# A two-layer graph network on one core: a written-out order of all operations is replaced by another

## The chip, the cores and the metric

The kernel runs on one core of a Trainium2 chip. The time is the device time of one execution in microseconds, the median of the runs shown. TensorE, VectorE, ScalarE, GpSimd and SyncE (DMA issues) each run their own instructions in the order in which the program gives them.

## The reference

The input x has 64 graphs of 256 nodes with 256 features, and adj an integer adjacency matrix of 256 x 256 for each graph. Two layers follow each other, and no graph meets another.

```
# layer 0: attention with relations
q, k = x@Wq + bq, x@Wk + bk                      # 8 heads of 32
attn = softmax(q @ k^T / sqrt(32))
out  = sum over r in 0..3 of (attn * (adj == r)) @ (x@Wv[r] + bv[r])
x = layernorm(x + out@Wo + bo)
x = layernorm(x + gelu(x@W1 + b1)@W2 + b2)       # 256 -> 1024 -> 256
# layer 1: two graph attentions, then feed-forward
for W, a in (W1', a1), (W2', a2):
    Wh = h@W;  e = leaky_relu(Wh@a[:256] + (Wh@a[256:])^T, 0.2)
    h = softmax(where(adj > 0, e, -9e15), axis=1) @ Wh
h = layernorm(x + h)
out = layernorm(h + relu(h@w_ff1 + b_ff1)@w_ff2 + b_ff2)
```

All arithmetic is float32.

## The kernel before, in words

One graph is one pass through 215 named operations, each a few instructions on one engine. A dictionary PLACES gives every operation of graph 0 a place, a number on an imaginary axis of microseconds; graph g has the same operations at PERIOD = 60 further on for each graph. All operations of all 64 graphs are sorted by place and written in that order (lines 738 to 743, under tc.manual_schedule()). So PLACES is nothing but an order: each engine executes its share of the sorted list one after the other, and the framework adds the waits that the data and the buffers need. A graph's places reach over several periods, so about seven graphs are in work at once: while one is read in, others are in attention, in the first feed-forward, in graph attention and in the second feed-forward.

The operations, by the letters that the text uses. A digit pair is group of four heads (m) and head (h) or chunk.

- load, cast, jT, mask0 to mask4, xT: x and adj are read by SyncE (five transfers), adj is cast on GpSimd, transposed by DMA, and compared with 0 to 3 (mask0 to mask3) and 0 (mask4) on GpSimd; x is transposed on VectorE.
- qk, v, s (TensorE) with qkc (ScalarE) and vc (VectorE): queries, keys and values, and scores, four heads at a time.
- max, rec (VectorE), exp, nrm (ScalarE): softmax of one head. eT (VectorE) transposes its 32 x 32 squares; eW writes them to DRAM and eR reads them back transposed, both issued by SyncE. ec (ScalarE) copies them to a PSUM bank (pe), pm (VectorE, 128 x 1536) and pl (GpSimd) multiply them by the masks. po (TensorE) is the product with the values, oT its copy; wo the output product, ya its sum with the residual, y and yb the residual's read and bias.
- st (VectorE), rt and nb (GpSimd), ln (ScalarE), and for norms 2 and 4 also lg, lb (GpSimd): layer norms 1 to 4.
- a.. and b.. are the two feed-forwards, called ffa and ffb: T, W, R transpose their input as eT, eW, eR do; u0 to u3 are the up products, x0 to x3 their activation on ScalarE, S1 to S4 differences of blocks on GpSimd, d1 to d7 the seven block products of the down matrix, e1, e5, e6, e7 and e their sums into the residual on VectorE, g and r the residual itself.
- hT, hW, hR (VectorE, SyncE, SyncE) transpose the first layer's result; ga0, ga1 (TensorE) are the first graph-attention product, gac0, gac1 their copies. ipA, zA, zmA, zxA, zeA, zdA are its scores, leaky rectifier, mask, maximum, exponential and division (zd is a reciprocal on VectorE and a scaling on ScalarE); h10, h11 the product, h1c its copies; ipB to zdB and h2, h2a the second attention.
- store writes the result.

Buffers are rings by tag. The products qk, v, po, wo, up, ga, ip, h1, h2 and d2 to d4 share two PSUM banks (tag mm, line 121), each free again when the operation that empties it is done. Four banks hold the scores, one pe, one the other four block products. The squares (tag sq) have three buffers, the transposed heads (eT) three.

Besides the graphs' operations three lists have places: the weights' reads on SyncE (LOAD_PLACE, one each LOAD_STEP), and the preparation of the weights of the first feed-forward, of the graph attention and of the second feed-forward (FFA_PLACE, GAT_PLACE, FFB_PLACE).

Of the kernel before, what the change touches and what calls it, by code (L numbers as in the profile page):

```python
# [25 lines left out]

PERIOD = 60.0
PLACES = {
    "load": 53.867, "cast": 97.493, "xT": 97.71, "qk0": 104.245, "qkc0": 106.9, "qk1": 119.672,
    "jT": 125.369, "qkc1": 125.559, "s0": 132.678, "max00": 140.518, "mask0": 141.136, "exp00": 142.758,  # L30
    "max01": 146.96, "max02": 148.02, "exp01": 150.777, "max03": 151.795, "exp02": 152.317,
    "rec00": 155.303, "exp03": 155.868, "v00": 155.904, "s1": 156.815, "rec01": 157.829, "rec02": 158.727,
    "nrm01": 159.842, "vc00": 160.216, "nrm02": 161.802, "max11": 161.859, "y": 164.73, "nrm00": 166.521,
    "eT01": 170.012, "max12": 170.188, "rec03": 171.372, "max13": 172.776, "nrm03": 173.676,
    "mask1": 174.748, "eT02": 174.962, "v01": 176.86, "eW01": 178.226, "mask2": 178.72, "exp11": 178.845,
    "exp13": 181.003, "vc01": 181.985, "eR01": 182.242, "eT03": 183.28, "eW02": 184.007, "max10": 184.378,
    "eR02": 184.784, "eT00": 185.682, "rec13": 186.046, "v10": 188.279, "exp12": 188.643, "rec11": 188.711,
    "exp10": 188.805, "mask3": 189.4, "rec12": 189.445, "nrm11": 189.698, "ec01": 190.244, "eW00": 190.751,
    "rec10": 192.438, "eT11": 193.076, "pm01": 193.141, "ec02": 193.235, "eR00": 193.339, "v11": 193.431,
    "vc10": 193.581, "vc11": 194.438, "pl02": 194.965, "nrm12": 198.135, "pm02": 198.356, "pl01": 198.886,  # L40
    "nrm10": 199.125, "eW03": 199.313, "ec00": 199.435, "pl00": 199.871, "eR03": 200.251, "eW11": 200.817,
    "nrm13": 201.713, "pm00": 203.767, "ec03": 203.968, "pm03": 204.13, "eT10": 204.663, "eR11": 205.899,
    "eT12": 206.287, "pl03": 206.79, "eW10": 209.302, "po0": 211.653, "eW12": 212.494, "eT13": 213.145,
    "mask4": 213.241, "oT0": 214.947, "eR10": 216.339, "pl11": 216.59, "ec11": 218.123, "pm11": 220.7,
    "eR12": 224.889, "yb": 226.434, "pl10": 228.258, "ec10": 228.372, "eW13": 229.644, "pm10": 230.476,
    "pl12": 232.012, "ec12": 232.733, "pm12": 233.972, "eR13": 234.313, "ec13": 237.646, "pm13": 243.245,
    "pl13": 244.342, "po1": 250.956, "oT1": 252.88, "wo": 255.663, "ya": 259.532, "st1": 263.955,
    "rt1": 267.947, "nb1": 268.416, "ln1": 268.951, "aT": 271.243, "ag": 274.747, "aW": 277.829,
    "aR": 278.673, "ar": 281.381, "au0": 286.043, "ax0": 287.596, "au1": 287.634, "ax1": 288.43,
    "au2": 290.21, "ax2": 291.522, "au3": 291.667, "aS1": 292.473, "ax3": 294.535, "ad1": 295.258,  # L50
    "aS2": 295.665, "aS4": 296.531, "ae1": 300.808, "aS3": 301.199, "ad5": 301.799, "ad2": 302.493,
    "ad3": 303.25, "ad6": 303.473, "ad4": 304.153, "ad7": 304.802, "ae6": 306.99, "ae": 307.007,
    "ae5": 310.654, "ae7": 310.829, "st2": 311.642, "rt2": 311.927, "nb2": 312.331, "ln2": 312.385,
    "lg2": 312.54, "lb2": 312.827, "hT": 316.295, "hW": 321.721, "hR": 322.436, "ga0": 324.446,
    "ga1": 327.351, "gac0": 327.988, "gac1": 328.62, "ipA": 328.64, "zA": 329.126, "zmA": 330.316,
    "zxA": 331.133, "zeA": 333.29, "zdA": 334.704, "h10": 336.089, "h1c0": 338.792, "h11": 340.441,
    "h1c1": 341.113, "ipB": 342.954, "zB": 344.83, "zmB": 345.246, "zxB": 345.394, "zeB": 347.408,
    "zdB": 348.854, "h2": 354.906, "h2a": 355.066, "st3": 359.521, "rt3": 359.942, "nb3": 360.337,
    "ln3": 361.345, "bT": 366.354, "bW": 370.407, "bR": 371.452, "bu0": 375.17, "bx0": 377.213,
    "bu1": 379.925, "bx1": 381.424, "bg": 381.467, "br": 381.616, "bu2": 381.993, "bu3": 382.236,  # L60
    "bS1": 382.83, "bx2": 383.199, "bd1": 383.914, "bx3": 385.532, "bd5": 387.758, "be1": 388.574,
    "bd2": 389.18, "bS2": 389.426, "bd3": 390.223, "bS4": 391.414, "bd4": 393.372, "be": 395.332,
    "bd6": 400.691, "bS3": 401.147, "be5": 401.254, "be6": 406.262, "bd7": 409.8, "be7": 410.516,
    "st4": 441.003, "rt4": 446.204, "nb4": 456.718, "ln4": 477.36, "lg4": 485.49, "lb4": 490.083,
    "store": 498.629,
}
LOAD_PLACE, LOAD_STEP = 122.0, 3.0
FFA_PLACE, GAT_PLACE, FFB_PLACE = 255.0, 262.0, 264.0

# [702 lines left out]
```

## Time and profile before

| | |
|---|---|
| median of 3 runs | 3732.0 us (3729.56 to 3735.53) |
| profiled execution | 3735.23 us, of which the span 3733.5 us |
| granted TensorE clock, mean | 0.982 |
| TensorE busy | 3527.7 us (94%) |
| GpSimd, VectorE, ScalarE busy | 2796.0, 2691.9, 2560.1 us |
| transfers | 457.94 MB, mean 123 GB/s |

The page of a profile counts the busy time of each engine over the whole span. Because the order is periodic, it is read best in one period of the middle: the timeline of each engine shows start, duration, the line of the kernel, the operation with its tiles, and in square brackets how long the engine stood idle before it and what ended that. The list of waits adds these up by pair: engine, line, what was waited for, total us, times, longest us. SPq is SyncE's queue of DMA issues; an L304 there is a write of squares (eW, aW, bW, hW), an L308 a read of them (eR, aR, bR), L320 is hR.

### The profile page before, as it was taken

Reading aid. Unit: us, or ns where it says so; the run is one execution under the profiler, and the core shown is the slowest. Engines: PE = TensorE matmul, PEld = TensorE weight load, DVE = VectorE, ACT = ScalarE, POOL = GpSimd, SP = SyncE. Lnnn points to the kernel's source line nnn. Section 1 sums busy time; section 2 is a strip of 40 time slices with the busy share of each in tenths; the row PEclk is TensorE's granted clock in tenths of the full one; section 3 lists DMA queues with packets and bytes.
Section 4 is the critical chain, followed back from the end, with each engine's and each line's share of the span. In section 5 each row is a group of like instructions: output and inputs, shape, how many; then the busy total and the mean of one; then the engine's idle time right before and its main releaser. Section 6 shows DMA issues by size and latency. Waiting matters only on the chain.

```text
span 3733.5 us, 72960 instructions
## 1 busy us (share of the span) xinstructions
PE 3527.7 (94%) x25944; PEld 2767.2 (74%) x25944; DVE 2691.9 (72%) x4756; ACT 2560.1 (69%) x6917; POOL 2796.0 (75%) x3014
## 2 busy tenths in 40 slices
PE   5799999999999999999999999999999999999985
PEld 3577777777777777777777777777777777777775
DVE  4677777777777777777777777777777777777752
ACT  4567677777667767767767767767777767767752
POOL 3477787787787787787787777777787787787774
PEclk8899999999999999999999999999999999999998
DMA  6434444444444444444444444444444444444320
GB/s 171 127 117 130 123 123 130 125 124 128 123 124 128 126 122 128 126 124 126 126 125 125 129 119 128 126 121 128 126 122 128 126 125 125 126 122 128 115 80 29
DMA packets 809885, 457.94 MB, mean 123 GB/s; under 512 B 334256, under 2 KB 718896, under 8 KB 809520
## 3 DMA queue, kind: packets, MB, share of 16 engines
q1 hardware_dynamic: 809520, 453.27, 41.1%
q8 instruction: 205, 3.36, 0.4%
q14 instruction: 160, 1.31, 0.1%
HBM read 243.42 MB, written 201.33 MB: 119 GB/s over the span
## 4 chain that ended last, share of the span: by engine, by line
PE 77%; DMA 10%; POOL 4%; DVE 3%; issue 2%; ACT 2%; SPq 2%; POOLq 0%; ACTq 0%; DVEq 0%
PE ffa_ps L380 11%; PE po L560 10%; PE v_ps L492 9%; DMA hT<-hT_d 7%; PE ffa_po L415 6%; PE qk_ps L473 6%; PE ffb_ps L380 5%; PE ffb_pq L415 5%; PE ffb_po L415 5%; PE ffa_pq L415 5%; PE ga_wps L590 4%; PE h_ps L635 3%; PE h_ps L649 3%; PE s L508 3%; DMA hT_d<-hT_sq 3%
## 5 line engine op out<-in xcount | busy, mean ns | idle before, releaser
L543 DVE TENSOR_TENSOR pm<-rel,pe 128x1536 f32<-128x1536 uint8 x512 | 892.4, 1743 | 212.2 <-ACT pe L539 162.5
L548 POOL TENSOR_TENSOR pl<-rell,eT 128x512 f32<-128x512 bf16 x512 | 589.3, 1167 | 164.2 <-PE po L560 112.0
L531 ACT ACTIVATE e<-e,rden 128x256 f32<-128x256 f32 x1024 | 455.6, 503 | 119.1 <-DVE rden L526 119.1
L492 PE MATMUL v_ps<-wv,xT 128*128 128x512 f32 x1024 | 490.9, 602 | 4.7 <-DVE v L499 3.4
L521 ACT ACTIVATE e<-s,nmax 128x256 f32<-128x256 f32 x1024 | 472.5, 477 | 22.9 <-DVE eT_sq L299 13.6
L380 PE MATMUL ffb_ps<-ffb_T,f 128*128 128x256 f32 x2048 | 465.8, 381 | 14.1 <-DMA ffb_T<-ffb_T_d 13.7
L380 PE MATMUL ffa_ps<-ffa_T,w 128*128 128x256 f32 x2048 | 463.7, 379 | 5.3 <-ACT ffa_h L388 5.3
L380 PEld LDWEIGHTS ffb_ps<-ffb_T,f 128*128 128x128 f32 x2048 | 390.4, 191 | 95.3 <-issue 43.8
L380 PEld LDWEIGHTS ffa_ps<-ffa_T,w 128*128 128x128 f32 x2048 | 383.7, 190 | 55.8 <-ACT ffa_h L388 6.3
L388 ACT ACTIVATE ffb_h<-ffb_ps,bf_c 128x256 f32<-128x256 f32 x512 | 217.1, 482 | 245.0 <-PE ffb_ps L380 244.9
L560 PE MATMUL po<-pm,v 128*32 128x256 f32 x6144 | 364.3, 385 | 18.5 <-DVE pm L543 17.9
L299 DVE STREAM_TRANSPOSE eT_sq<-e 128x512 f32<-128x512 f32 x512 | 350.3, 694 | 16.5 <-DMA eT_d<-eT_sq 14.4
L403 POOL TENSOR_TENSOR ffa_t<-ffa_h 128x512 f32<-128x512 f32 x64 | 81.8, 1278 | 371.6 <-ACT ffa_h L388 371.6
L513 DVE TENSOR_REDUCE nmax<-s 128x2 f32<-128x512 f32 x512 | 335.1, 664 | 6.0 <-PE s L508 6.0
L539 ACT COPY pe<-eT 128x512 f32<-128x512 f32 x512 | 304.8, 595 | 41.5 <-DVE pm L543 19.0
L560 PEld LDWEIGHTS po<-pm,v 128*32 128x32 f32 x6144 | 188.0, 111 | 190.3 <-issue 51.8
L357 ACT ACTIVATE ffa_res<-ffa_res,nb_x,rs_x 128x256 f32<-128x256 f32 x256 | 139.8, 593 | 238.7 <-POOL nb_x L352 238.7
L465 POOL TENSOR_SCALAR rel<-adT 128x512 uint8<-128x512 bf16 x192 | 289.0, 1506 | 12.0 <-DMA adT<-adb 12.0
L492 PEld LDWEIGHTS v_ps<-wv,xT 128*128 128x128 f32 x1024 | 175.4, 191 | 151.7 <-issue 124.6
L423 DVE TENSOR_TENSOR ffb_res<-ffb_po,ffb_res 128x256 f32<-128x256 f32 (+2 forms) x256 | 133.2, 521 | 207.6 <-PE ffb_po L415 140.1
L499 DVE TENSOR_TENSOR v<-v_ps,bv_r 128x512 f32<-128x512 f32 x256 | 176.5, 689 | 128.9 <-PE v_ps L492 122.9
L590 PE MATMUL ga_wps<-gext,hT 128*128 128x260 f32 x512 | 138.2, 416 | 110.0 <-DMA hT<-hT_d 110.0
(140 smaller groups left out, 7965.8 us busy)
## 6 DMA issues: line engine op xcount, KB each, us to landing
eT_d<-eT_sq SPq DMA_DIRECT2D x512, 256.0 KB, 2.3
eT<-eT_d SPq DMA_DIRECT2D x512, 256.0 KB, 3.1
xin<-in_x_dram SPq DMA_DIRECT2D x256, 64.0 KB, 3.6
adi<-in_adj_dram SPq DMA_DIRECT2D x64, 256.0 KB, 3.2
y<-in_x_dram SPq DMA_DIRECT2D x64, 256.0 KB, 3.2
ffa_T_d<-ffa_T_sq SPq DMA_DIRECT2D x64, 256.0 KB, 2.0
ffa_T<-ffa_T_d SPq DMA_DIRECT2D x64, 256.0 KB, 2.8
hT_d<-hT_sq SPq DMA_DIRECT2D x64, 256.0 KB, 3.2
```

The costliest lines, as they stand in the source:

```text
L299: nc.vector.transpose(self.sq.rearrange("p a c k y -> p (c k) a y"), src.rearrange("p c (k a x) -> p (c k) a x", k=KD, a=A))
L380: nc.tensor.matmul(p[:, f - f0, :], self.wa[:, k, f * P:(f + 1) * P], self.x.nodes(k), start=(k == 0), stop=(k == KD - 1))
L415: nc.tensor.matmul(self.p[bank][:, k], a[:, f], seven[self.name[:3]][i][:, f], start=(f == 0), stop=(f == KF // 2 - 1))
L465: nc.gpsimd.tensor_scalar(t.rearrange("p b c k y -> p (c k) b y"), self.adT.rearrange("p c k (b y) -> p (c k) b y", b=A), float(r), None, ...
L492: nc.tensor.matmul(p, self.xT[:, k, jc * P:(jc + 1) * P], wv[:, k, m].rearrange("p r n -> p (r n)"), start=(k == 0), stop=(k == KD - 1))
L513: nc.vector.tensor_reduce(self.nmax[m, h], self.s4[m][h].rearrange("p (c n) -> p c n", c=C), AX.X, ALU.max, negate=True)
L521: nc.scalar.activation(e[:, ic, :], self.s4[m][h][:, ic * N:(ic + 1) * N], AF.Exp, bias=self.nmax[m, h][:, ic:ic + 1], accum_out=self.den[ ...
L531: nc.scalar.activation(e[:, ic, :], e[:, ic, :], AF.Copy, scale=self.rden[m, h][:, ic:ic + 1])
L539: nc.scalar.copy(self.pe[m, h], self.et[m, h].t.rearrange("p b c k y -> p (b c k y)"))
L543: nc.vector.tensor_tensor(self.pm[m, h], self.rel.rearrange("p r b c k y -> p r (b c k y)"), bc(self.pe[m, h], [P, R - 1, C * N]), ALU.mult)
L548: nc.gpsimd.tensor_tensor(self.pm_l[m, h], self.rel_l.rearrange("p b c k y -> p (b c k y)"), self.et[m, h].t.rearrange("p b c k y -> p (b ...
L560: nc.tensor.matmul(po[hp, :], self.v[m][:, jc, r, hp], w, start=(r == 0 and jc == 0), stop=(r == R - 1 and jc == C - 1))
```

## The change

Only numbers change: the places of all operations, and those of the weights' reads and preparations. PERIOD stays at 60. The change is described as places found anew from a model in which transfers land in order and reads wait in SyncE's queue for their writes. The block products of the feed-forward (d1 to d7), which that description names too, are in both versions. From a graph's load to its store the places reach from 53.9 to 498.6 before and from 50.5 to 468.5 after. The core of the diff:

```diff
...
 PERIOD = 60.0
 PLACES = {
-    "load": 53.867, "cast": 97.493, "xT": 97.71, "qk0": 104.245, "qkc0": 106.9, "qk1": 119.672,
...
-    "nrm10": 199.125, "eW03": 199.313, "ec00": 199.435, "pl00": 199.871, "eR03": 200.251, "eW11": 200.817,
...
-    "eT12": 206.287, "pl03": 206.79, "eW10": 209.302, "po0": 211.653, "eW12": 212.494, "eT13": 213.145,
...
-    "aS2": 295.665, "aS4": 296.531, "ae1": 300.808, "aS3": 301.199, "ad5": 301.799, "ad2": 302.493,
...
-    "lg2": 312.54, "lb2": 312.827, "hT": 316.295, "hW": 321.721, "hR": 322.436, "ga0": 324.446,
-    "ga1": 327.351, "gac0": 327.988, "gac1": 328.62, "ipA": 328.64, "zA": 329.126, "zmA": 330.316,
-    "zxA": 331.133, "zeA": 333.29, "zdA": 334.704, "h10": 336.089, "h1c0": 338.792, "h11": 340.441,
-    "h1c1": 341.113, "ipB": 342.954, "zB": 344.83, "zmB": 345.246, "zxB": 345.394, "zeB": 347.408,
-    "zdB": 348.854, "h2": 354.906, "h2a": 355.066, "st3": 359.521, "rt3": 359.942, "nb3": 360.337,
-    "ln3": 361.345, "bT": 366.354, "bW": 370.407, "bR": 371.452, "bu0": 375.17, "bx0": 377.213,
...
-    "bS1": 382.83, "bx2": 383.199, "bd1": 383.914, "bx3": 385.532, "bd5": 387.758, "be1": 388.574,
...
+    "load": 50.469, "cast": 57.958, "jT": 95.84, "xT": 96.554, "mask0": 102.911, "mask1": 110.047,
...
+    "eR01": 157.633, "rec00": 157.8, "nrm00": 158.594, "eT00": 159.275, "nrm02": 159.922, "v01": 160.652,
...
+    "eW02": 170.328, "max10": 170.786, "nrm03": 171.325, "pl01": 171.348, "nrm11": 171.556, "eR00": 171.905,
+    "eT03": 172.223, "exp13": 172.85, "ec01": 172.891, "v10": 173.717, "vc10": 175.654, "rec12": 176.645,
+    "eT11": 177.037, "eW03": 177.436, "exp10": 178.092, "pm01": 178.674, "ec00": 179.248, "v11": 179.856,
+    "rec10": 180.535, "eR02": 180.538, "vc11": 180.966, "pl00": 182.451, "nrm10": 182.861, "pm00": 183.232,
+    "eT10": 184.014, "eR03": 184.212, "ec02": 186.356, "eW11": 186.418, "rec13": 187.778, "pm02": 188.384,
...
+    "eT12": 201.973, "mask4": 201.982, "oT0": 202.206, "pm11": 203.952, "eW13": 204.473, "eR10": 205.839,
...
+    "ln2": 296.499, "lg2": 298.191, "lb2": 298.532, "hT": 301.25, "hW": 306.094, "hR": 310.927,
+    "ga0": 312.907, "ga1": 313.044, "gac0": 313.944, "gac1": 314.043, "ipA": 315.499, "zA": 316.936,
+    "zmA": 319.507, "zxA": 320.243, "zeA": 321.567, "zdA": 321.6, "h10": 324.214, "h11": 324.414,
...
+    "zeB": 349.157, "zdB": 349.403, "h2": 349.965, "h2a": 351.453, "st3": 351.613, "rt3": 352.789,
+    "nb3": 353.038, "ln3": 354.94, "bT": 355.146, "bW": 357.939, "bR": 359.837, "bu0": 363.297,
...
+    "be": 384.147, "bS3": 385.351, "be1": 386.889, "bd6": 388.841, "bd7": 396.301, "be6": 396.573,
...
+    "lb4": 465.278, "store": 468.471,
...
-LOAD_PLACE, LOAD_STEP = 122.0, 3.0
-FFA_PLACE, GAT_PLACE, FFB_PLACE = 255.0, 262.0, 264.0
+LOAD_PLACE, LOAD_STEP = 97.0, 3.0
+FFA_PLACE, GAT_PLACE, FFB_PLACE = 253.0, 305.0, 308.0
```

What these numbers mean is seen when the places are taken modulo 60: the order that repeats in each period. In the lists below, worked out from the diff, the number after the point is the whole number of periods in the place: in period n the operation with .k is that of graph n - k. So two operations with different numbers belong to different graphs, and from the end of the list to its start the number of the same graph rises by one.

```
TensorE, before:
  ad5.5 ad2.5 ad3.5 ad6.5 ad4.5 ad7.5 v10.3 po1.4 s0.2 v11.3 bu0.6 wo.4 bu1.6 bu2.6 bu3.6 bd1.6
  ga0.5 ga1.5 bd5.6 ipA.5 bd2.6 bd3.6 po0.3 bd4.6 v00.2 h10.5 s1.2 h11.5 bd6.6 ipB.5 qk0.1 au0.4
  au1.4 bd7.6 au2.4 au3.4 h2.5 ad1.4 v01.2 qk1.1
TensorE, after:
  qk1.2 s0.2 bu0.6 bu1.6 bu2.6 bu3.6 bd1.6 ga0.5 ga1.5 bd5.6 ipA.5 po0.3 bd2.6 bd3.6 bd4.6 h10.5
  h11.5 v00.2 bd6.6 ipB.5 au0.4 au1.4 bd7.6 s1.2 au2.4 au3.4 v01.2 ad1.4 po1.3 ad5.4 ad6.4 h2.5
  ad2.4 ad3.4 ad4.4 ad7.4 v10.2 wo.3 qk0.1 v11.2
SyncE (DMA issues), before:
  eR01.3 eW02.3 eR02.3 jT.2 bW.6 eW00.3 bR.6 eR00.3 store.8 eW03.3 eR03.3 eW11.3 hW.5 hR.5 eR11.3 eW10.3
  eW12.3 eR10.3 aW.4 aR.4 y.2 eR12.3 eW13.3 load.0 eR13.3 eW01.2
SyncE (DMA issues), after:
  eR02.3 eR03.3 hW.5 eW11.3 hR.5 eR11.3 eW10.3 y.3 aW.4 eW13.3 eR10.3 aR.4 eW12.3 eR13.3 eR12.3 eW01.2
  jT.1 eR01.2 store.7 eW00.2 eW02.2 load.0 eR00.2 eW03.2 bW.5 bR.5
VectorE, after:
  st1.4 rec10.3 vc11.3 hT.5 pm00.3 eT10.3 rec13.3 pm02.3 aT.4 pm03.3 max01.2 eT13.3 max00.2 max02.2 zmA.5 zxA.5
  be5.6 zdA.5 eT12.3 rec01.2 max03.2 pm11.3 be.6 be1.6 vc00.2 pm10.3 zmB.5 eT01.2 rec02.2 pm13.3 zxB.5 xT.1
  be6.6 rec00.2 be7.6 pm12.3 eT00.2 eT02.2 max12.2 rec03.2 max11.2 st4.6 vc01.2 zdB.5 max13.2 rec11.2 ae1.4 max10.2
  ae6.4 h2a.5 st3.5 eT03.2 ae5.4 ae.4 ae7.4 st2.4 bT.5 vc10.2 rec12.2 eT11.2 ya.3 pm01.2
ScalarE, after:
  nrm10.3 qkc1.2 bx0.6 ec02.3 bx1.6 ln1.4 bx2.6 ec03.3 bx3.6 nrm13.3 gac0.5 gac1.5 ec11.3 zA.5 nrm12.3 exp01.2
  zeA.5 zdA.5 oT0.3 ln4.7 exp02.2 h1c0.5 nrm01.2 ec10.3 h1c1.5 exp00.2 zB.5 exp03.2 ec13.3 ax0.4 ax1.4 ec12.3
  ax2.4 nrm00.2 nrm02.2 ax3.4 exp12.2 zeB.5 exp11.2 zdB.5 oT1.3 nrm03.2 nrm11.2 exp13.2 ec01.2 ln3.5 ln2.4 exp10.2
  qkc0.1 ec00.2
GpSimd, after:
  pl00.3 rt1.4 bg.6 nb1.4 pl02.3 br.6 bS1.6 pl03.3 rt4.7 nb4.7 bS2.6 bS4.6 mask4.3 bS3.6 pl11.3 lg4.7
  ag.4 mask2.2 yb.3 pl10.3 mask3.2 pl13.3 pl12.3 mask0.1 aS1.4 aS2.4 ar.4 lb4.7 aS4.4 aS3.4 mask1.1 pl01.2
  rt3.5 nb3.5 rt2.4 nb2.4 cast.0 lg2.4 lb2.4
```

## The prediction

> **What bounds the kernel now.** I read the busy table first, then the waits of TensorE, then one period on each engine, then the ends of the span.
>
> ```profile
> PE 3527.7 (94%) x25944; PEld 2767.2 (74%) x25944; DVE 2691.9 (72%) x4756; ACT 2560.1 (69%) x6917; POOL 2796.0 (75%) x3014
> ...
> PE ga_wps L590 <- DMA hT<-hT_d: 110.0, 64, 9.0
> PE po L560 <- DVE pm L543: 17.9, 3, 9.2
> PE s L508 <- ACT e L521: 15.3, 4, 14.7
> ...
> 276.00:332.00 56.00, 54.34 (x405) 42.83 (x406) 42.20 (x76) 39.84 (x108) 43.95 (x48) 1.00 0.43 127
> ```
>
> TensorE is the bound: in a 56 us stretch of the middle it is busy 54.3, GpSimd 44, VectorE 42, ScalarE 40. It waits once per graph, always in the same place (64 times): the first product of the graph attention, ga0, waits for the transposed rows hT. All its other waits together are below that and lie at the two ends. Now one period, TensorE first, then the chain that makes hT, then SyncE's queue (SP):
>
> ```profile
> 1206.70 1.06 PE L415 MATMUL ffa_po<-w,ffa_h 128*128 128x128 f32 x8
> 1207.60 1.88 PE L492 MATMUL v_ps<-wv,xT 128*128 128x512 f32 x4
> ...
> 1226.80 1.99 PE L590 MATMUL ga_wps<-gext,hT 128*128 128x260 f32 x8 [1.22 <-DMA hT<-hT_d]
> ...
> 1209.90 0.75 DVE L340 BATCH_NORM_STATS2 st_x<-ffa_res 128x6 f32<-128x256 f32 x2
> ...
> 1212.63 1.09 ACT L357 ACTIVATE ffa_res<-ffa_res,nb_x,rs_x 128x256 f32<-128x256 f32 x2 [2.12 <-POOL nb_x L352]
> ...
> 1215.16 1.27 POOL L327 TENSOR_TENSOR ffa_res<-ffa_res,be_r 128x512 f32<-128x512 f32 x1
> ...
> 1216.70 0.70 DVE L299 STREAM_TRANSPOSE hT_sq<-ffa_res 128x512 f32<-128x512 f32 x1
> ...
> 1218.71 0.36 SPq L308 DMA_DIRECT2D eT<-eT_d  x1
> 1219.17 0.44 SPq L304 DMA_DIRECT2D eT_d<-eT_sq  x1
> 1219.66 0.43 SPq L304 DMA_DIRECT2D hT_d<-hT_sq  x1
> 1222.88 0.67 SPq L320 DMA_DIRECT2D hT<-hT_d  x1
> ```
>
> TensorE leaves ad7, the last block product of the first feed-forward, at 1207.6 (where the next matmul starts) and gets to ga0 18.0 us later. The chain ad7, st2, ln2, lb2, hT, hW, hR, ga0 takes 19.2. Its squares are ready at 1217.4, but hW goes out at 1219.66: SP stands behind an eR (1218.71) that waits for a buffer which GpSimd's pl frees, and an eW. Those 2.3 us are more than the whole wait. Undisturbed periods are 55.6 us; from ga0 at 220.65 to ga0 at 3520.59 are 59 periods, 55.93 on average, because in a few the wait reaches 2.6 us and the clock then drops.
>
> **What the Trainium skill says.** "DMA: Bandwidth & Descriptors", section "Two DMAs through the same engine are not ordered", says that the issuing engine must wait for the first transfer's semaphore before it issues one that reads what the first wrote. So a read blocks all of SP until its write has landed; here hW to hR is 3.2 us, and an unhurried pair (ffb_T, 1205.56 to 1207.97) 2.4. The same page, "Anatomy of one DMA", puts some 2.0 us fixed on a transfer; the trace has 2.0 to 3.9. "TensorE: Matmul & The Clock Gate", section "HAM oscillation", warns of idle gaps over about 3.4 us; here a gap of 2.61 us (ga0 at 1002.59) was already followed by a stretch at 0.83, so the measurement decides.
>
> **The change part by part.** No instruction is added or removed; all that changes is the order on each engine. I rank the places modulo 60, which gives each engine's order in one period, and walk it with start-to-start times from this trace. Let t be zero when TensorE leaves ad7. Pitches on TensorE: v 1.72, wo, qk, h2 and each up product 1.73, s 1.07, po 3.59, block product 0.89, ga0 with ga1 1.83, h10 or h11 0.97, ip 0.22. They sum to 53.6 per period; the trace without its wait has 55.57 - 1.42 = 54.15, so 0.5 are small gaps that I keep.
>
> *hT.* On TensorE the new order between ad7 and ga0 is v10, wo, qk0, v11, qk1, s0, four up products, bd1: 1.72+1.73+1.73+1.72+1.73+1.07+6.92+0.89 = 17.5 us, against 18.0 before, so the cover is no longer. The chain: ae7 ends 0.6, st2 1.6, root and offset (1.63) 3.3, ln2 4.4, lg2 and lb2 (1.24 each) 7.1. hT stands in VectorE's queue behind bT, vc10, eT11, ya, pm01 (1.67), st1 and vc11; vc11 waits for v11 (6.9 + 0.2) and ends 7.8, so hT ends at 8.4, sooner than before (9.8). The gain is in SP: before hW come bW (2.5), bR (4.9, after bW landed), eR02 and eR03 (5.3, 5.7), all gone by 6.1. hW goes at 8.5, behind nothing; hR 2.4 to 3.2 later, lands 3.9 on (this read's row): 14.8 to 15.6. ga0 is wanted at 17.5. **The wait goes, with 1.9 to 2.7 us to spare.**
>
> *bR, moved in front of hW.* bT needs ln3 (ends 1.1) and st2; bR lands 2.8 after 4.9, at 7.7; the first up product bu0 is wanted at 9.7 (before: much later). No wait, 2 us of slack.
>
> *The ring of two PSUM banks (tag mm).* Every product takes a bank that an evacuation two products earlier frees. Along the new order: qk0 (3.45) needs vc10, done 3.0; qk1 (6.9) needs qkc0, which stands behind ln2 and exp10, done 6.1; bu2 (13.2) needs bx0, 12.4; v01 (40.4) needs ax2, 39.6; h10 (26.7) needs zdA, 25.4; h2 (48.3) needs zdB, 46.7. One is late: **h11** (27.7) needs be, the add that empties the bank of bd2 to bd4. On VectorE be stands behind the reciprocal of zdA, eT12, rec01, max03 and pm11. ga0 ends 18.4; gac1 and ec11 by 20.3, zA 21.5, zmA and zxA 23.0, zeA (behind nrm12 and exp01) 24.2, reciprocal 24.4, eT12 25.0, max03 25.7, pm11 27.4, be 28.0. So TensorE waits about 0.35 us, and v00, bd6 and ipB behind it. Bounds: 0 if exp01 and nrm12 have run before zA, 1.0 if pm11 or zeA comes 0.7 later. I take 0.35. GpSimd's mask0 now waits for pm12 (40.0), which leaves pl01 at 51.7 and rt3 just on time (51.9): no cost, but no slack.
>
> So a period is 54.15 + 0.35 = 54.5: 59 x (55.93 - 54.5) = **84 us**. The low end without that wait is 59 x 1.78 = 105.
>
> *Fill.* The products ahead of the first ga0 are the same set before and after. In the chain of waits the preparation of the attention and second feed-forward weights stands alone from 97.8 to 117.7, 20 us (GAT_PLACE 262, FFB_PLACE 264). At 305 and 308 it falls between hT and ga0 of graph 0, where TensorE waited 9.0 us (165.39). I take that 9 as gain; bounds 17 (SP also comes to the first eW some 5 us sooner, as one group of loads less is ahead of it) and a loss of 5, if the new place holds up ga0. *Drain.* From the last hT on (3670.6 to 3733.5) one graph is alone and its chain is latency; two shorter slots before it may give 2. LOAD_PLACE: every weight is issued 25 places sooner, still ahead of its first use: nothing.
>
> Sum: 84 + 9 + 2 = 95 from the profiled execution's 3735.2 (span 3733.5 and 1.7 around it): 3640. The median of the three runs is 3.2 lower, 3732.0: so **3637**.
>
> **The rivals.**
> *Half given back.* Slacks of 0.45 (qk0 behind vc10), 0.75 (qk1 behind qkc0) and 0 (rt3) are as small as my latencies are rough; if 1.0 us more goes to such waits, the period is 55.5 and the time 3735 - 25 - 11 - 3 = 3696. For it: pm waits for pe 162.5 us in 192 places already. Against: in the walk VectorE idles 5 us between t = 10 and 24, which absorbs delays.
> *hT still late.* If SP is held at bR, eR02 or eR03 until hW goes at 12 (12 + 3.0 + 3.9 = 18.9 against 17.5), ga0 waits as before: 3732. Against: bT is ready by 2.3, and the buffers of both eR are free long before.
> *Slower: VectorE's queue takes the bound.* If zeA, and so everything through be, comes 2.5 us later than walked, h11 stops TensorE 2.85 us per period: 57.0, 59 x 1.07 = 63 lost, 11 gained at the ends, 3784. It decides from 1.8 us of stall at h11, where it equals what hT gives back. For it: ec02 is queued behind bx0, and pm02, pm03, max01 and zmA follow one another. Against: be would have to come 1.4 us later than the rows say.
>
> **How the numbers follow.** Forecast 0.62, half given back 0.15, hT still late 0.06, slower 0.17. A measurement of this kernel tells 0.2%, 7 us, from no change. Faster 0.77, same 0.06, slower 0.17. Range: the low end is 105 + 17 + 3 from 3732, 3607, and a little for clock drops that vanish: 3603; the high end takes in half given back and hT still late, 3736.
>
> **What would show it.** Right: ga0's wait for hT gone from TensorE's waits, periods of 54.2 to 54.9, hW's issue within 0.5 us of hT's end, a wait of some tenths at h11 (h_ps) on VectorE's ffb_res, first ga0 before 160. Wrong: 64 waits of over 1 us at any one TensorE line, above all h_ps, qk_ps or ffb_ps; periods over 55.9.

## The result and the profile after

The kernel after takes 3642.4 us (median of 4 runs, 3637.9 to 3643.7), the kernel before 3730.8 on the same chip (4 runs, 3728.2 to 3735.5): a ratio of 0.976, 95% interval 0.974 to 0.978, or 88 us. The profiled execution has 3637.9 us with a span of 3636.1; before these were 3735.2 and 3733.5.

The busy table of the kernel after, engine by engine:

```profile
PE 3537.1 (97%) x25944; PEld 2759.8 (76%) x25944; DVE 2685.0 (74%) x4756; ACT 2565.8 (71%) x6917; POOL 2795.3 (77%) x3014
```

The same instructions on every engine, in a span 97 us shorter. Now TensorE's waits of the kernel after (engine, line, what was waited for, total us, times, longest):

```profile
PE ffb_ps L380 <- DMA ffb_T<-ffb_T_d: 24.9, 4, 10.5
PE po L560 <- DVE pm L543: 15.5, 5, 5.4
PE qk_ps L473 <- DMA wq<-in_L_gnn_Wq_dram: 7.7, 1, 7.7
PE v_ps L492 <- DVE v L499: 7.5, 1, 7.5
PE s L508 <- ACT e L521: 5.7, 4, 2.8
```

ga0 no longer waits for hT; that row (110.0 us, 64 times) is gone from the list. What is left occurs one to five times, at the two ends. One period of the kernel after, from one ga0 to the next, in the table of stretches (TensorE, weight loads, VectorE, ScalarE, GpSimd):

```profile
1190.00:1244.68 54.68, 54.56 (x406) 42.75 (x405) 41.75 (x75) 39.94 (x109) 43.65 (x48) 1.00 0.43 129
```

TensorE is busy 54.56 of 54.68 us; the missing 0.12 is one gap, which is followed up below. The timeline of the same period shows the chain that used to be late, by engine:

```profile
1226.99 1.88 PE L492 MATMUL v_ps<-wv,xT 128*128 128x512 f32 x4
...
1244.68 1.92 PE L590 MATMUL ga_wps<-gext,hT 128*128 128x260 f32 x8
...
1234.69 0.70 DVE L299 STREAM_TRANSPOSE hT_sq<-ffa_res 128x512 f32<-128x512 f32 x1
...
1229.26 0.33 SPq L304 DMA_DIRECT2D ffb_T_d<-ffb_T_sq  x1
1231.32 0.37 SPq L308 DMA_DIRECT2D ffb_T<-ffb_T_d  x1
1231.78 1.01 SPq L308 DMA_DIRECT2D eT<-eT_d  x2
1235.42 0.33 SPq L304 DMA_DIRECT2D hT_d<-hT_sq  x1
...
1237.49 0.64 SPq L320 DMA_DIRECT2D hT<-hT_d  x1
```

TensorE leaves ad7 at 1226.99, the squares hT are ready at 1235.39, and hW goes out 0.03 us later. hR follows 2.07 us after hW and lands 4.1 us on, at 1241.6 (the median of this read is 3.8); ga0 takes it at 1244.68 with 3.0 us to spare, 3.3 in the median of 59 periods. Before, hW stood 2.3 us behind a read and a write.

The table compares all kernels of this study. The first two columns after the ratio are the starts of ga0 of graphs 0 and 1 in the trace, then the mean period over the next 59 graphs, then the time from ga0 of graph 60 to the end of the span. Each kernel is named by the experiment below.

| kernel | median us | ratio to before, 95% interval | ga0, graph 0 | graph 1 | period | rest |
|---|---|---|---|---|---|---|
| before | 3730.8 | | 165.4 | 220.7 | 55.93 | 212.9 |
| after | 3642.4 | 0.976 [0.974, 0.978] | 148.1 | 205.7 | 54.68 | 204.1 |
| e1_hw_early | 3658.0 | 0.981 [0.979, 0.982] | 162.0 | 215.5 | 54.71 | 207.4 |
| e9_zA_alone | 3731.2 | 1.001 [1.000, 1.001] | 163.3 | 218.6 | 55.94 | 209.8 |
| e7_hw_and_zA_early | 3611.4 | 0.968 [0.967, 0.969] | 161.2 | 215.0 | 53.98 | 209.7 |
| e10_hw_zA_weights | 3607.6 | 0.968 [0.967, 0.969] | 156.9 | 215.6 | 53.98 | 208.3 |
| e2_weights_late | 3724.8 | 0.999 [0.998, 1.000] | 156.4 | 216.6 | 55.85 | 209.3 |
| e3_both | 3655.7 | 0.980 [0.979, 0.982] | 156.1 | 214.6 | 54.74 | 210.7 |
| e5_weights_early | 3647.5 | 0.978 [0.976, 0.979] | 161.2 | 214.8 | 54.69 | 206.1 |
| e8_loads_late | 3637.6 | 0.975 [0.974, 0.976] | 147.8 | 205.9 | 54.68 | 206.1 |
| e6_hw_behind_eR11 | 3669.9 | 0.984 [0.982, 0.985] | 149.2 | 207.4 | 55.06 | 208.3 |
| e4_ae5_early | 3619.7 | 0.971 [0.970, 0.973] | 148.1 | 205.9 | 54.32 | 207.5 |
| e11_be_early | 3635.0 | 0.975 [0.974, 0.977] | 149.3 | 207.5 | 54.54 | 207.7 |
| e12_ae5_be_early | 3613.0 | 0.969 [0.968, 0.971] | 148.8 | 206.5 | 54.18 | 208.8 |

### The profile page after: what moved, and what is told of

Its sections match the earlier page's. It is cut to its first block, busy times and chain, and to the rows that moved or that the text cites. A ratio compares the mean times of both kernels' runs of the same rounds, so it can differ in the third digit from the quotient of the medians.

```text
span 3636.1 us, 73240 instructions
## 1 busy us (share of the span) xinstructions
PE 3537.1 (97%) x25944; PEld 2759.8 (76%) x25944; DVE 2685.0 (74%) x4756; ACT 2565.8 (71%) x6917; POOL 2795.3 (77%) x3014
## 4 chain that ended last, share of the span: by engine, by line
PE 95%; DMA 1%; DVE 1%; issue 1%; SPq 1%; ACT 1%; POOL 0%; POOLq 0%; ACTq 0%; DVEq 0%
PE ffb_ps L380 13%; PE po L560 12%; PE ffa_ps L380 12%; PE v_ps L492 12%; PE ffa_po L415 7%; PE ffb_po L415 6%; PE qk_ps L473 6%; PE ffb_pq L415 5%; PE ffa_pq L415 5%; PE s L508 4%; PE h_ps L635 3%; PE h_ps L649 3%; PE ga_wps L590 3%; PE wo_ps L580 3%; DMA eT<-eT_d 0%
## 5 line engine op out<-in xcount | busy, mean ns | idle before, releaser
L380 PEld LDWEIGHTS ffb_ps<-ffb_T,f 128*128 128x128 f32 x2048 | 388.2, 192 | 98.1 <-issue 43.9
L465 POOL TENSOR_SCALAR rel<-adT 128x512 uint8<-128x512 bf16 x192 | 287.3, 1497 | 215.9 <-DVE pm L543 183.7
L357 ACT ACTIVATE ffa_res<-ffa_res,nb_x,rs_x 128x256 f32<-128x256 f32 x256 | 139.7, 593 | 403.6 <-POOL nb_x L352 403.6
L388 ACT ACTIVATE ffb_h<-ffb_ps,bf_c 128x256 f32<-128x256 f32 x512 | 215.0, 471 | 210.5 <-PE ffb_ps L380 210.5
L492 PEld LDWEIGHTS v_ps<-wv,xT 128*128 128x128 f32 x1024 | 190.2, 191 | 144.5 <-issue 125.6
L388 ACT ACTIVATE ffa_h<-ffa_ps,b_c 128x256 f32<-128x256 f32 x512 | 207.3, 471 | 112.3 <-PE ffa_ps L380 111.6
L499 DVE TENSOR_TENSOR v<-v_ps,bv_r 128x512 f32<-128x512 f32 x256 | 172.4, 673 | 148.8 <-PE v_ps L492 148.7
L423 DVE TENSOR_TENSOR ffa_res<-ffa_po,ffa_res 128x256 f32<-128x256 f32 (+2 forms) x256 | 131.1, 512 | 190.6 <-PE ffa_po L415 183.7
L346 POOL TENSOR_SCALAR rs_x<-mv_x 128x2 f32<-128x2 f32 x256 | 56.9, 222 | 223.3 <-DVE mv_x L342 212.5
```

What stands on the lines that cost most here:

```text
L380: nc.tensor.matmul(p[:, f - f0, :], self.wa[:, k, f * P:(f + 1) * P], self.x.nodes(k), start=(k == 0), stop=(k == KD - 1))
L388: nc.scalar.activation(self.h[half][:, f1 + f, :], self.ps[f0][:, f, :], self.func, bias=self.ba[:, f0 + f:f0 + f + 1])
L492: nc.tensor.matmul(p, self.xT[:, k, jc * P:(jc + 1) * P], wv[:, k, m].rearrange("p r n -> p (r n)"), start=(k == 0), stop=(k == KD - 1))
```

## The experiments

The theory: ga0 waited because of SyncE's queue, not because of the work before it, and the 88 us are that wait less what the new order adds in smaller waits, and a shorter fill. The rivals: TensorE's order or the other queues made the gain; or the gain lies in the fill.

### hW alone in the old order

```diff
 before:
-"hT": 316.295, "hW": 321.721
+"hT": 316.295, "hW": 320.2
```

> The old order with one number changed: hW's place from 321.721 to 320.2, so SyncE issues the write of hT's squares ahead of the read eR03 (which waits for GpSimd's pl) and of the write eW11, not behind them. Theory (the wait at ga0 is made in SyncE's queue): hW goes out at once after hT, some 2 us sooner; hR then lands about 1 us before TensorE wants it; TensorE's wait for hT falls from 110 us to under 20, periods from 55.6 to 54.2, and the time from 3731 to between 3625 and 3655. Rival (the wait belongs to the chain of norm, GpSimd and VectorE, and only the whole new order mends it): ga0 still waits over 1 us per graph and the time stays within 10 us of 3731.

It took 3658.0 us: 71 of the change's 88 us from one number. The wait of ga0 for hT fell to 10.0 us in 3 graphs. The time is still a little above what was expected, and TensorE's waits name the reason:

```profile
PE po L560 <- ACT ga_z L609: 32.6, 59, 0.6
PE po L560 <- DVE pm L543: 17.4, 3, 8.4
```

po0 now waits in 59 graphs for the PSUM bank that zA empties. In the timeline of ScalarE and TensorE:

```profile
1258.10 1.09 ACT L357 ACTIVATE y<-y,nb_x,rs_x 128x256 f32<-128x256 f32 x2 [1.06 <-POOL nb_x L352]
1259.10 0.81 ACT L609 ACTIVATE ga_z<-ga_ips,ga_wh 128x256 f32<-128x256 f32 x2
...
1259.96 2.37 PE L560 MATMUL po<-pm,v 128*32 128x256 f32 x40 [0.44 <-ACT ga_z L609]
```

zA (L609) could start at 1257.7, when ipA ends, but stands in ScalarE's queue behind ln1 of another graph (L357), which itself waits 1.06 us for GpSimd. This is the wait that took the place of the one removed.

### zA alone, and with hW

```diff
 before:
-"ipA": 328.64, "zA": 329.126
+"ipA": 328.64, "zA": 328.7
```

> The kernel before with zA alone moved, from 329.126 to 328.7, so ahead of ln1 of the graph before on ScalarE; hW stays where it was. Theory: two limits lie one behind the other. While ga0 waits 1.4 us for hT in every graph, po0 has no wait that zA's place could take away, so nothing changes: 3722 to 3738, the wait of ga0 for hT stays at about 110 us. With hW moved as well the same edit was worth 46 us (3658 to 3611). Rival: ScalarE's order has a worth of its own, because everything behind zA comes 1 us sooner: 3690 to 3715.

Nothing changed: 3731.2 against 3728.9 for the kernel before on that chip. TensorE's waits have the old row:

```profile
PE ga_wps L590 <- DMA hT<-hT_d: 110.6, 64, 8.9
```

The same edit with hW's:

> The kernel before with two operations moved: hW from 321.721 to 320.2 (as in e1_hw_early, 3658) and zA from 329.126 to 328.7, ahead of ln1 of the graph before on ScalarE. In e1_hw_early po0 waited 0.55 us in 59 graphs for the PSUM bank that zA empties. Theory: ln1 in front of zA made that wait; with zA first it goes, 59 x 0.55 = 32 us: 3622 to 3632, period 54.1 to 54.3. ln1 then comes 0.5 us later, which nothing near needs. Rival: zA itself is late because ipA and the copies gac are, and po0 still waits 0.4 us or more, or the wait moves to the next product of the ring (bd2 for the bank of po0's other user): 3640 to 3660.

3611.4 us, 47 less than with hW alone and lower than the whole change by 31. The period is 53.98. The timeline shows why, zA now ahead of ln1:

```profile
1243.42 0.84 ACT L609 ACTIVATE ga_z<-ga_ips,ga_wh 128x256 f32<-128x256 f32 x2 [0.73 <-PE ga_ips L602]
1244.15 1.08 ACT L357 ACTIVATE y<-y,nb_x,rs_x 128x256 f32<-128x256 f32 x2
...
1245.10 2.80 PE L560 MATMUL po<-pm,v 128*32 128x256 f32 x48
```

and the table of stretches has no idle TensorE any more:

```profile
400.00:1000.00 600.00, 600.00 (x4476) 473.47 (x4475) 466.14 (x827) 444.53 (x1203) 484.73 (x522) 1.00 0.43 130
```

The size was underestimated: 59 x 0.55 = 32 us were expected, 59 x (54.71 - 53.98) = 43 came. po0's weight loads are late too, by up to 0.8 us (43.9 us in 59 graphs in the list of the kernel with hW alone), so the wait costs more than its 32.6 us. So two limits lay one behind the other, and the second was invisible until the first was gone: its edit is worth nothing alone and 47 us after the other.

### The weights' preparation and the weights' reads

```diff
 before:
-FFA_PLACE, GAT_PLACE, FFB_PLACE = 255.0, 262.0, 264.0
+FFA_PLACE, GAT_PLACE, FFB_PLACE = 255.0, 319.6, 319.7
```

> The old order with only the preparation of the graph attention's and the second feed-forward's weights moved: GAT_PLACE 262 to 319.6, FFB_PLACE 264 to 319.7, between hT and ga0 of graph 0. Theory (in the fill they stood alone on the chain for 20 us, and here fall into the 9 us wait for hT): the first ga0 comes 9 to 17 us sooner than 165.4, and the time falls by the same, to between 3712 and 3723; the steady periods stay at 55.6. Rival (the new place holds up ga0 by as much as the old one cost): the first ga0 between 160 and 170 and a time of 3726 to 3736.

The first ga0 came 9.0 us sooner, as forecast, the second only 4.0: about half is given back within one graph. In the time it is 4 us against the kernel before on that chip (3728.7), less than the theory expected and a little more than the rival did. The same edit with hW:

> The old order with both: hW at 320.2, GAT_PLACE 319.6, FFB_PLACE 319.7. Theory (the two parts act in different stretches and add up): the gain is the sum of those of the two single kernels within 5 us, 3610 to 3645, which would be as fast as the whole new order or faster. Rival (the weights' preparation now delays the sooner hT in the fill, so the second gain is lost): the time of the kernel with hW alone, within 4 us.

3655.7, only 2.3 below hW alone: the time is the rival's, the two don't add. The first ga0 is 5.8 us sooner than with hW alone, but the second only 1.0, so here too most is given back within one graph. And on top of hW and zA:

> The kernel before with hW at 320.2, zA at 328.7 and the preparation of the graph-attention and second feed-forward weights moved from 262 and 264 to 319.6 and 319.7, between hT and ga0 of graph 0. Theory: the first ga0 comes 5 us sooner (161 to 156), of which the next graph gives most back, as in e3_both, where it was worth 2.3 us: 3605 to 3611 against 3611 without it. Rival: with the steady part free of waits the whole 5 us stay: 3603 to 3606.

3607.6 (3605.1 to 3610.7) against 3611.4 (3609.9 to 3611.7): the second ga0 is no sooner (215.6 against 215.0), the ratios agree; the 4 us are not settled. It is the lowest median of this study. Then the reverse in the new order:

```diff
 after:
-FFA_PLACE, GAT_PLACE, FFB_PLACE = 253.0, 305.0, 308.0
+FFA_PLACE, GAT_PLACE, FFB_PLACE = 253.0, 258.0, 260.0
```

> The kernel after, with GAT_PLACE and FFB_PLACE back at 258 and 260, that is before the first feed-forward of graph 0 and not between its hT and ga0. If the new place of the weights' preparation is what brought the first ga0 from 165.4 to 148.1, the first ga0 comes 9 to 15 us later, 157 to 163, and the steady period stays at 54.7. Theory: about half of it is given back by the second ga0 (as 5 of 9 us were in the old order), so the total is 3645 to 3652, 0.1 to 0.25% above the kernel after (3642). Rival 1: all of it stays, 3651 to 3657. Rival 2: the place doesn't matter, because the earlier start of the whole pipeline gave the gain: first ga0 within 2 us of 148, total 3640 to 3645.

13.2 us later at the first ga0, 9.1 at the second: a part is given back within one graph, as the theory has it. At the ga0 of graph 60 it is still 9.5. The median is 5.2 us above the kernel after, which is inside the forecast, but the intervals of the two ratios overlap; between 5 and 10 us, what is left of it in the time is not settled. The reads alone:

```diff
 after:
-LOAD_PLACE, LOAD_STEP = 97.0, 3.0
+LOAD_PLACE, LOAD_STEP = 122.0, 3.0
```

> The kernel after with LOAD_PLACE back at 122, so that SyncE issues the weights' reads 25 places later; nothing else changes. In the old order the weights' preparation was worth 9 us at the first ga0, but the kernel after is 17.3 us sooner there; the other 8 are either the order of the operations or these reads. Theory (order): first ga0 at 147 to 150, total 3638 to 3646. Rival (reads): first ga0 5 to 9 us later, 153 to 157, total 3645 to 3652.

First ga0 at 147.8, time 3637.6: 4.8 below the kernel after, on another chip. The starts, the period and the rest differ by at most 2 us in the traces and the intervals of the ratios overlap, so no cost and no gain of the reads' place is shown.

### hW held in the new order

```diff
 after:
-"hT": 301.25, "hW": 306.094, "hR": 310.927
+"hT": 301.25, "hW": 312.2, "hR": 312.5
```

> The kernel after, with hW and hR put at 312.2 and 312.5: in SyncE's queue hW then stands behind eW11 and behind eR11, which can't be issued before eW11's squares have landed (2.1 to 3.2 us after eW11). Everything else keeps its order. Theory (the head of SyncE's queue decides when hT lands): hW 2.5 to 3.5 us later than hT's end, hR lands about that much later; of it 3.4 us of slack before ga0 are used up first, so ga0 waits 0 to 1 us per graph, and 59 periods give 0 to 60 us: 3640 to 3700, likeliest 3665, with a wait of TensorE's ga0 for hT in 20 to 64 graphs. Rival (hT has much more slack than 3.4 us, or SyncE's order isn't the cause): no waits for hT, 3638 to 3645.

3669.9, close to the likeliest 3665, with the wait back in 22 graphs:

```profile
PE ga_wps L590 <- DMA hT<-hT_d: 12.5, 22, 2.2
```

SyncE's queue in one period, where hT ended at 1241.78, and the ga0 that follows:

```profile
1239.27 0.45 SPq L304 DMA_DIRECT2D eT_d<-eT_sq  x1
1243.53 0.36 SPq L308 DMA_DIRECT2D eT<-eT_d  x1
1243.93 1.78 SPq L304 DMA_DIRECT2D hT_d<-hT_sq  x1
1247.80 0.64 SPq L320 DMA_DIRECT2D hT<-hT_d  x1
...
1251.59 1.99 PE L590 MATMUL ga_wps<-gext,hT 128*128 128x260 f32 x8 [0.35 <-DMA hT<-hT_d]
```

The read eR11 can't go before eW11 has landed (in the trace its wait ends with that, at 1243.40) and holds everything behind it for 3.8 us; hW goes 2.15 us after hT, and hR 3.87 after hW instead of 2.07. Landing 3.7 later, at 1251.5, it holds ga0 until 1251.59: the slack is used up. The period grows by 0.38, 22 us over 59. Only 12.5 are listed as this wait, but all of it lies at ga0: from the start of bd1 to that of ga0 59 periods take 71.7 us, against 52.6 in the kernel after, and ga0 with ga1 106.8 against 103.6. In 50 of the 59 ga0 starts within 0.3 us of hT's landing; in the kernel after it does so in none. The kernel keeps the new order otherwise, so it is the place in SyncE's queue that decides.

### The waits that the new order brings

The trace shows two places in each period at which TensorE starts late in the kernel after. The first is the last block product of the first feed-forward, ad7, in the timeline of TensorE, of its weight loads and of VectorE; the last line is ad4 of the kernel before, where ad7 follows at 1206.70:

```profile
1224.85 1.06 PE L415 MATMUL ffa_pq<-w,ffa_t 128*128 128x128 f32 x8
1226.03 1.13 PE L415 MATMUL ffa_po<-w,ffa_h 128*128 128x128 f32 x8
...
1226.00 0.97 PEld L415 LDWEIGHTS ffa_po<-w,ffa_h 128*128 128x128 f32 x8 [0.28 <-issue]
...
1225.50 0.38 DVE L423 TENSOR_TENSOR ffa_res<-ffa_po,ffa_res 128x256 f32<-128x256 f32 x1
...
1205.81 1.06 PE L415 MATMUL ffa_pq<-w,ffa_t 128*128 128x128 f32 x8
```

From ad4 to ad7 it is 1.18 us, where it was 0.89 before, the pitch of a block product. The add ae5 ends at 1225.88; ad7's loads start at 1226.00. ae5 reads another quarter of ad7's PSUM bank, and in the program ad7's first product carries a wait on VectorE. The trace calls the gap "issue" here, but in graph 0, here of the kernel with the weights early, it is long enough to be named (in the kernel after at 126.36, also 0.25 us):

```profile
145.77 1.13 PE L415 MATMUL ffa_po<-w,ffa_h 128*128 128x128 f32 x8 [0.25 <-DVE ffa_res L423]
```

The Trainium skill, "PSUM — Partial Sum Buffer", section "PSUM bank collisions raise a hardware error", gives a likely reason for such a wait: two engines must not access the same 32 partitions of one bank at once, even at different addresses, so a bank is guarded with its partitions and not by address. ad7 and ae5 both take all 128 partitions. No run here shows a collision; that the wait costs time, the next one does. ae5 needs ad5 only, which is long done; it stands behind h2a, st3 and eT03. So it was put ahead:

```diff
 after:
-"ae5": 292.42, "ad4": 292.531
+"ae5": 291.2, "ad4": 292.531
```

> The new order with one number changed: ae5's place from 292.42 to 291.2, so VectorE reads block product 5 out of the shared bank ahead of h2a and st3. Theory (in the new order d7 waits about 0.3 us per graph for ae5, since both use one PSUM bank): the start-to-start time from ad4 to ad7 falls from 1.18 to 0.9 us, periods from 54.68 to 54.4, the time by 15 to 18 us from 3642 to about 3625. Rival (d7 waits for the sum ae or the difference aS3, or h2a and its norm now come later by as much and qk0 waits instead): periods stay at 54.6 to 54.8 and the time within 5 us of 3642.

3619.7, 22.6 below the kernel after. The timeline of this kernel:

```profile
1218.54 1.06 PE L415 MATMUL ffa_pq<-w,ffa_t 128*128 128x128 f32 x8
1219.43 1.06 PE L415 MATMUL ffa_po<-w,ffa_h 128*128 128x128 f32 x8
```

0.89 again. 15 to 18 us were expected from the 0.29 alone; but ad7 itself also took 0.96 to the next product and now takes 0.89, so the wait was worth 0.36, the whole difference of the periods (54.68 to 54.32), 21 us. The longer product points to the weight loads: the first of ad7's eight matmuls takes 0.18 us to the next in the kernel after, each other one 0.11. The Trainium skill, "TensorE: Matmul & The Clock Gate", section "Step-by-step: what each phase is for", says that TensorE pulls a weight load ahead while the product before it still runs. A product that waits has lost that lead: ad7's loads start at 1226.00, 0.03 us ahead of it. That this is the reason was not tried apart from the wait.

The second place is h11, where the prediction put its wait. The list of waits of the weight loads has it:

```profile
PEld h_ps L635 <- DVE ffb_res L423: 19.6, 61, 0.3
```

and the timeline of TensorE has it at the first products of h10 and h11:

```profile
1199.33 0.38 PE L635 MATMUL h_ps<-ga_wh,ga_z 128*128 128x258 f32 x1
...
1200.29 0.48 PE L635 MATMUL h_ps<-ga_wh,ga_z 128*128 128x258 f32 x1
```

Four products of 0.22 would put h11 at 1200.21; it starts 0.08 later, and its first product takes 0.32 to the next (1200.61) instead of 0.22. h10 with h11 takes 1.93 us instead of 1.74. So be was moved ahead of pm11:

```diff
 after:
-"be": 384.147
+"be": 383.94
```

> The kernel after with the add be moved on VectorE from 384.147 to 383.94, that is ahead of pm11 and no longer behind it; nothing else moves. In the kernel after the weight loads of h11 wait 0.33 us for be in 61 graphs, and h11's four products start 0.09 us late and take 0.1 us longer: h10 with h11 takes 1.93 us instead of 1.74. Theory: that is the whole price of h11's wait; with be first it goes, 59 x 0.19 = 11 us: 3626 to 3636 against 3642, period 54.5. VectorE then stands 1.3 us before be for the last block product, and pm11 comes 1.8 us later, into a stretch where VectorE idles 2.2 us. Rival 1: the wait of the loads lies beside other work and costs nothing: 3638 to 3646. Rival 2: pm11's delay reaches the evacuation of v00 or the next heads and costs more than it gives: over 3646.

3635.0, 7.4 below the kernel after; the period falls by 0.14, h10 with h11 by the same (1.93 to 1.79). The loads still wait 0.2 us (11.2 us in 61 graphs). The wait is a cost, a little below the 11 us expected. Both edits:

> The kernel after with both edits: ae5 at 291.2 (as in e4_ae5_early, 3620) and be at 383.94 (as in e11_be_early). Theory: the two waits lie in different stretches of the period and add: 22 and 11 us below 3642, 3604 to 3612, period 54.1. Rival: with both gone another wait appears, as after hW's move, and only 22 to 26 us are left: 3616 to 3620.

3613.0: 29.4 below the kernel after, where the single edits gave 22.6 and 7.4. They add within the noise, as two waits in different stretches of the period should. The theory's sum (33) was 3 to 4 us too high because be gave less, so the time lies 1 us above its range; the rival's further wait did not appear. This version is as fast as the old order with hW and zA moved (3611.4), within 2 us; both beat the two kernels compared.

## Why the prediction was right, and where it was not

Forecast were 3637 us, measured are 3642.4. The sum was 84 + 9 + 2, for periods, fill and drain. The two profiled executions, which lie 97 us apart, give 74 + 15 + 9; the medians lie 88 apart, which leaves 14 for the two ends. So the mechanism was right, and that the total is only 5 us off is in part luck: the periods gave 10 us less than forecast, and the ends at least 3 more.

*hT and SyncE.* Right in mechanism and in nearly every time. Counted from the moment TensorE leaves ad7, hT ends at 8.4 (forecast 8.4), hW goes at 8.4 (8.5), hR at 10.5 (10.9 to 11.7), ga0 comes at 17.7 (17.5). The slack is 3.3 us against 1.9 to 2.7: write to read took less than the lower end of the range. Moving hW alone, and holding it in the new order, show that the queue is the cause.

*bR in front of hW.* Right: bW goes at 2.3, bR at 4.3, and bu0 at 9.8 does not wait.

*The ring and h11.* Right in place, wrong in size and in how it shows. be ends at 27.9 (forecast 28.0), but TensorE gets to h11 at 27.9, not 27.7, because of small gaps ahead of it, so at most 0.19 us was lost and not 0.35; and it appears in the waits of the weight loads, not in those of the products, where the prediction said one should look. mask0 waits for pm12 on GpSimd as walked, 3.2 us in 58 graphs (183.7 us in the list of waits), and costs nothing.

*What the walk missed.* The walk checked each product against the evacuation that frees its bank. It left out ad7, which opens no bank but waits on the add ae5 that reads its neighbour in the same one: 0.36 us per graph, 21 us in all. This is the term that was left out. The period forecast without any wait was 54.15, the measured one is 54.68. Of the 0.53 between them 0.36 is ad7; the other 0.17 is spread over joins of about 0.1 us, where one group of products follows another. The wait at h11, for which the prediction added 0.35, adds nothing to its base: it took 0.97 each for h10 and h11 from the old order, 1.94 together, and in the new order the two take 1.93. That 54.68 lies so near the forecast 54.5 is again in part luck: an expected 0.35 did not come and an unforeseen 0.53 did.

*The fill.* Mis-sized: 9 us from the place of the weights' preparation, measured 13.2 at the first ga0 and 9.1 at the second in the new order. The rest of the 17.3 and 14.9 is about what hW alone gives at these two in the old order (3.4 and 5.1); for the new order this is not shown, since holding hW back there delays them by 1.1 and 1.7 only. That part is given back in the next graph was not foreseen; it held in both orders. *The drain* (2 forecast) is 8.7 in the two profiled executions, but the rest of the span differs by up to 5.5 us among kernels of one order: the seven of the new order have a mean of 207.0, the seven of the old 209.7, so 3 is the better figure. *The reads of the weights:* nothing, as forecast.

*The rivals.* Half given back, with a period of 55.5, did not happen, but a weaker form of it did: against the old order with hW and zA moved, the new order runs 54.68 - 53.98 = 0.70 us slower per period, 41 us of the steady part; half of it is ad7 (0.36), the rest is spread over joins of about 0.1 us. h11 has no part in it, since h10 with h11 takes 1.94 us there too. hT still late and VectorE as the bound did not happen: VectorE is busy 42 of 54.7 us and h11 loses at most 0.2, far from the 1.8 from which the change would lose.

## What to carry to other kernels

When a single wait recurs in every period, find which queue holds the last link of its chain, and move that one instruction before anything else: one number gave 71 of 88 us, and a second one, worthless by itself, gave 47 more. After each wait that goes, read the list again, that of the weight loads too: two waits of 0.3 us there, which did not appear among the products' waits, gave back 0.36 and 0.14 us per period when the add in question was moved. When an order is checked by hand, check every product against every reader of its PSUM bank, not only against the one that frees it.

## What the runs showed of the hardware

A short wait of TensorE costs more than the idle time that the timeline shows. Block products are drawn 1.06 us long and follow each other every 0.89, so the drawn spans overlap by 0.17 us; the 0.12 us of idle time before ad7 is a start 0.29 late. And the first matmul after a wait takes longer to the next one: 0.18 us at ad7 where the others take 0.11, and 0.30 at a ga0 that waited for hT (1226.80 in the kernel before) where it is 0.22 at one that did not (1244.68 in the kernel after). So 0.12 us of idle time at ad7 cost 0.36.

The clock can fall with no gap just before. In the kernel after, TensorE does the weights' preparation right before the first ga0. After gaps of 0.89 and 0.78 us the trace grants half the clock from 141.1 to 144.5, then the full clock to 147.9, while 32 products with a single column each run, then half of it again to 151.3, where ga0 runs. Table of stretches, the clock granted being the third number from the end:

```profile
144.00:148.00 4.00, 4.00 (x34) 3.83 (x32) 0.50 (x2) 0.06 (x1) 0.00 (x0) 0.93 0.00 0
148.00:152.00 4.00, 3.67 (x10) 2.59 (x9) 3.66 (x7) 3.12 (x4) 0.00 (x0) 0.59 0.00 0
```

TensorE counts as busy all through 144 to 148, and yet ga0 then runs at 0.59 and takes 3.58 us instead of 1.92. The second fall follows no gap but a stretch that held the single-column products alone; with ae5, be, both or hW moved in the new order the traces have the same sequence. No run changed these products, so that they are the reason is not shown.
